# Where the first cross attention's vector work stands in order, and when the third expert weights are loaded

## The chip, the cores and the metric

The kernel runs on one core of one Trainium2 chip. The metric is device time in microseconds (us). An execution that is profiled also leaves a trace: for each engine, which instruction ran when. The engines are PE (TensorE, matrix products; PEld is its loading of weights), DVE (VectorE), ACT (ScalarE), POOL (GpSimd) and SP (SyncE, which here only issues DMAs). Each engine works through its own list of instructions, in an order that is fixed when the program is built.

## The reference: what is computed

Eight batches of 256 tokens with 256 features go through four blocks. Each block adds a gated cross attention to a context and then a gated feed-forward part:

```python
x = x + tanh(g_xattn[i]) * xattn_i(layernorm(x), ctx, ...)
x = x + tanh(g_ffn[i])   * ffn_i(layernorm(x), ...)
```

Block 0 has a cosine attention and a dense feed-forward part. Block 1 is the one that matters here: an attention of 16 heads with 16 features each, with the masked rows of the normalized input set to zero, and then a mixture of 8 experts. A router product gives 8 scores per token, the two greatest are kept, their exponentials are divided by their sum (the gates), and each kept expert computes `silu(x W1) * (x W2)`, 682 wide, times `W3`. Block 2 has an attention of 16 heads with 64 features and another mixture of 8 experts, with two shared experts beside it. Block 3 has two attentions.

## The kernel before

`x` stays on the chip, 16 tiles of 128 tokens (two tiles to a batch). The blocks follow one another.

**The attention of 16-wide heads** is `attention16` (L502), called for block 1 with `prologue` and `epilogue` from L813 and L837. It is a pipeline over 32 steps, four to a batch; a step does four heads. Step n, in the order of the code: `greatest` (L536) multiplies keys by queries (L525, tile `lg`) and has DVE take the greatest logit of each row, negated (L544, tile `nms`, two instructions); then the generators of the next batch's prologue and of the earlier batches' epilogues each advance by one `yield`; in every second step `shift` transposes the maxima (L556) and adds them to the queries (L558); `weights` multiplies again for a step three earlier (L525, tile `lb`) with the exponential on ACT (L570); and `values` multiplies by the values (L586) for a step four earlier. The logits, the second logits and the projections share three PSUM buffers (`psum2`, L49), so the second logits of a step wait until DVE has read the first ones.

The **prologue** of a batch has four parts: normalize x and transpose it (`ln_T`, L241: sums L207 and L208, variance L198, power -1/2 on POOL L200, row mask L219, apply L223, transposes L238 with ACT's copy L239); the queries (L675, DVE L822); the keys (ACT L828); the values (L685, ACT L689). The **epilogue** of a batch (from L837) begins four steps after the batch's last `greatest`: transposes (L606) and division by the row sums (`normalized`, L725 and L729), the residual (L841), the sums for the next norm (`norm_stats`); then `moe_token` (L735): the norm's apply and the store of the normalized tokens to DRAM by SP (L738), their transposes, the router product (L747, L751); then the two greatest scores (`top2_mask`, L755 to L770), and in a further step the gates (`l1_gates`, L778 to L787 and L801).

**Who sets the order.** The code's order is not the order of the lists. A planner in the tile framework simulates the program when it is built: on each engine it takes the earliest instruction of the code that is ready by its own estimate. An instruction that depends on little may so move ahead of others that stand before it in the code. The block `with behind(kind):` (L191) limits that: every instruction that the block issues on the engine of `latest[kind]` is put behind that instruction in the list. It adds no wait. `latest["maxima"]` is the last L544, `latest["norm"]` the last power on POOL. The second and the fourth attention use `behind` already, the first doesn't.

**The mixture of block 1** (L1069 to L1121). `places` (L858) makes from the mask, by a chain of small DVE instructions and three matrix products, the list of tokens for each of 39 slots of 128: first the place of each token, then one-hot rows (L925, four of them) whose products with PE (L930) give `token` (L935, L936), then the expert of each slot (L940 to L947). `l1_gates` for the last batch and `two_gates` (L959 to L973) make the two gates of each token. `routed` (L975) gathers the tokens of a slot with indirect DMAs from POOL (L982), transposes them (L992), multiplies by W1 and W2 (L1088), gates (ACT L1096, DVE L1098), transposes (L1009) and multiplies by W3 (L1106). W1 is loaded at the kernel's start (L109). W2 and W3 lie in a pool that is opened after the attention, so their DMAs on SP (L1071, L1074) wait until the attention's tiles are free. Block 2's mixture uses the same `places` and `two_gates`, with its shared experts' products beside them.

Of the kernel before, what the change touches and what calls it, by code (L numbers as in the profile page):

```python
# [8 lines left out]
F32 = mybir.dt.float32  # L9
# [26 lines left out]
def flamingo_kernel(ctx: ExitStack, tc: tile.TileContext, out: bass.AP, a: dict):  # L36
    nc = tc.nc

    const = ctx.enter_context(tc.tile_pool(name="const", bufs=1))
    w01_stack = ctx.enter_context(ExitStack())  # L40
    w01 = w01_stack.enter_context(tc.tile_pool(name="w01", bufs=1, side="right"))
    dram = ctx.enter_context(tc.tile_pool(name="dram", bufs=1, space=bass.MemoryType.DRAM))
# [79 lines left out]
    def gf(i):  # L122
        return gates[:, 4 + i : 5 + i]
# [37 lines left out]
        out=trip, in_=trip, compare_op=ALU.is_gt, fill=0.0, base=0,  # L161
        pattern=[[1, P]], channel_multiplier=-1,
    )
    count_i = const.tile([P, P], I32, name="count_i")
    nc.gpsimd.iota(count_i, pattern=[[1, P]], base=0, channel_multiplier=0)
    count = const.tile([P, P], F32, name="count")
    nc.vector.tensor_copy(count, count_i)
# [23 lines left out]
    def behind(kind):  # L191


        return tc.issue_after(latest[kind].ins)
# [16 lines left out]
    def norm_stats(b, name):  # L211
        mv = stats_of(x[:, 2 * b : 2 * b + 2, :], 2, name)
        return mv, rstd_of(mv, 2, name)
# [27 lines left out]
    def ln_T(b, name, rowmask=None):  # L241
        xn = layer_norm(b, name, rowmask)
        t = lnp.tile([P, 2, S], F32, tag="xnT", name=f"xnT_{name}")
        transposed(xn, t, name)
        return t
# [559 lines left out]
    with tc.tile_pool(name="l1x", bufs=2) as pl, tc.tile_pool(name="l1x1", bufs=1) as pl1:  # L805
        wq, wk, wv = l1x_w
        maskf = pl1.tile([P, NT], F32, name="maskf")
        nc.vector.tensor_copy(maskf, mask_u8)
        vas = spread_tiles(pl1, "l1")
        maxima = cleared_maxima(pl1, "l1")  # L810
        gcol = gx(1)

        def prologue(b):  # L813

            cx = ctx01[:, :, b * S : (b + 1) * S]
            xnT = ln_T(b, f"l1x{b}", rowmask=maskf[:, 2 * b : 2 * b + 2])
            qT = pl.tile([P, 4, S], F32, tag="qT", bufs=3, name=f"l1q{b}")
            kT = pl.tile([P, 4, S], F32, tag="kT", bufs=3, name=f"l1k{b}")
            yield
            for _, pp in project(wq, 2, lambda c: xnT[:, c, :], 2, f"l1pq{b}"):  # L820
                for u in range(2):
                    nc.vector.tensor_scalar(  # L822
                        of_half(qT, u), pp[:, 0:2, :], quarter[:, u : u + 1], None, ALU.mult
                    )
            yield
            for _, pp in project(wk, 2, lambda c: cx[:, c, :], 2, f"l1pk{b}"):
                for u in range(2):
                    nc.scalar.activation(  # L828
                        of_half(kT, u), pp[:, 0:2, :], AF.Identity,
                        bias=one_a[:, u : u + 1], scale=half[:, u : u + 1],  # L830
                    )
            yield
            va = vas[b % 3]
            values16(wv, lambda c, k: cx[:, c, k * P : (k + 1) * P], va, f"l1pv{b}")
            yield qT, kT, va

        def epilogue(b, av, st):  # L837
            att = pl.tile([P, 2, D], F32, tag="att", name=f"l1att{b}")
            normalized(av, 16, H, att, f"l1n{b}")
            xb = x[:, 2 * b : 2 * b + 2, :]  # L840
            nc.vector.scalar_tensor_tensor(xb, att, gcol, xb, ALU.mult, ALU.add)  # L841
            stats = norm_stats(b, f"l1f{b}")
            yield
            xT = lnp.tile([P, 2, S], F32, tag="xnT", name=f"xnT_l1f{b}")
            yield from moe_token(b, stats, l1xd, xT, l1_s, l1f_wg, "l1f")
            ts = slice(2 * b, 2 * b + 2)
            top2_mask(l1_s[:, ts, :], l1_mask[:, :, ts], f"l1g{b}", moe)
            if b + 1 < B:
                yield
                l1_gates(ts, f"l1g{b}")  # L850

        attention16("l1", pl, maxima, prologue, epilogue)

# [4 lines left out]
    def places(mask, name, pl1, kept):  # L858
# [63 lines left out]
        for k in range(4):  # L922
            ts = slice(k * NT // 2, (k + 1) * NT // 2)
            row = pl1.tile([P, NT // 2, P], BF16, tag=f"{name}row", name=f"{name}row{k}", bufs=2)
            nc.vector.tensor_tensor(  # L925
                row, count.unsqueeze(1).to_broadcast([P, NT // 2, P]),
                rc[:, 0, ts].unsqueeze(2).to_broadcast([P, NT // 2, P]), ALU.is_equal,
            )
            for t in range(k * NT // 2, (k + 1) * NT // 2):
                nc.tensor.matmul(  # L930
                    pi[:, : 2 * SP], row[:, t % (NT // 2), :], what[:, t].rearrange("p k s -> p (k s)"),
                    start=t == 0, stop=t == 2 * NT - 1,
                )
# [3 lines left out]

        at = pl1.tile([P, SP, E], F32, name=f"{name}at")
        edge = pl1.tile([P, E], F32, name=f"{name}edge")
        nc.vector.tensor_scalar_mul(edge, first[:, 0, :], 1.0 / P)  # L940
        nc.vector.tensor_tensor(
            at, edge.unsqueeze(1).to_broadcast([P, SP, E]),
            count[:, :SP].unsqueeze(2).to_broadcast([P, SP, E]), ALU.is_le,
        )
        expert_f = pl1.tile([P, SP], F32, name=f"{name}expert_f")
        nc.vector.tensor_reduce(expert_f, at, AX.X, ALU.add)
        nc.vector.tensor_scalar_add(expert, expert_f, -1.0)  # L947
        return slot, two

    def kept_tiles(pool, name):  # L950
# [115 lines left out]
    l1_kept = kept_tiles(const, "l1")  # L1066
    l1yd = dram.tile([SLOTS * P, D], F32, name="l1yd")
    l2x_pool, l2x_w = ExitStack(), {}
    with tc.tile_pool(name="l1w", bufs=1, side="right") as plw:  # L1069
        l1_w2 = plw.tile([P, E, 2, HID], F32, name="l1_w2")  # L1070
        nc.sync.dma_start(out=l1_w2, in_=a["l1f_w12"][:, :, :, HID:])  # L1071
        l1_w3 = plw.tile([P, E, NHC, D], F32, name="l1_w3")
        for e0 in range(0, E, 4):
            nc.sync.dma_start(out=l1_w3[:, e0 : e0 + 4], in_=a["l1f_w3"][:, e0 : e0 + 4])  # L1074
        l1_w12 = (l1_w1, l1_w2)
        token, expert, two_i, g2 = l1_kept
        with tc.tile_pool(name="l1p", bufs=1, side="right") as plp:
            slot, two = places(l1_mask, "l1g", plp, l1_kept[:3])
            l1_gates(slice(NT - 2, NT), "l1g_last")
            two_gates(l1_gate, slot, two, gf(1), g2, "l1g", plp)  # L1080
        with tc.tile_pool(name="l1f", bufs=2, side="right") as pl:
            def first_half(s, xT, e):
                ph = [psum2(f"l1ph{s}_{k}") for k in range(2)]
                for k in range(2):
                    for n in range(2):
                        o = n * HH
                        for c in range(2):
                            nc.tensor.matmul(  # L1088
                                ph[k][:, n, :HH], xT[:, c, :],
                                l1_w12[k][:, bass.ds(e, 1), c, o : o + HH].rearrange(  # L1090
                                    "p o n -> p (o n)"
                                ),
                                start=c == 0, stop=c == 1,
                            )
                sl = pl.tile([P, 2, HH], F32, tag="sl", name=f"l1sl{s}", bufs=1)
                nc.scalar.activation(sl, ph[0][:, :, :HH], AF.Silu)  # L1096
                h = pl.tile([P, HID], F32, tag="h", name=f"l1h{s}")
                nc.vector.tensor_tensor(  # L1098
                    h.rearrange("p (n h) -> p n h", n=2), sl, ph[1][:, :, :HH], ALU.mult
                )  # L1100
                return h

            def second_half(po, hT, e):
                for f in range(NHC):
                    n = min(P, HID - f * P)
                    nc.tensor.matmul(  # L1106
                        po, hT[:n, f, :],
                        l1_w3[:n, bass.ds(e, 1), f, :].rearrange("p o n -> p (o n)"),
                        start=f == 0, stop=f == NHC - 1,
                    )  # L1110

            def halfway():

                l1a_stack.close()
                pool = l2x_pool.enter_context(tc.tile_pool(name="l2x1", bufs=1))
                for n in ("l2x_wk", "l2x_wv", "l2x_wq", "l2x_wo"):
                    l2x_w[n] = load_w(n, pool)

            routed(
                l1xd, l1yd, token, expert, first_half, second_half, NHC, pl, "l1", halfway  # L1120
            )  # L1121


    l2w_stack = ctx.enter_context(ExitStack())
# [75 lines left out]
    with tc.tile_pool(name="l2r", bufs=1) as pl1, ExitStack() as l2s_stack:  # L1200
# [17 lines left out]
        pls = l2s_stack.enter_context(tc.tile_pool(name="l2s", bufs=2))  # L1218
        with tc.tile_pool(name="l2p", bufs=1) as plp:
            slot, two = places(mask2, "l2g", plp, l2_kept[:3])  # L1220
            nc.vector.tensor_tensor(gate2, gate2, mask2.rearrange("p e t -> p t e"), ALU.mult)
            two_gates(gate2, slot, two, gf(2), g2, "l2g", plp)


        l3x_w = [load_w(n, l3q) for n in ("l3x_wq", "l3x_wk", "l3x_wv", "l3x_wo")]
# [593 lines left out]
```

## Time and profile before

| what | us |
|---|---|
| median of 3 runs (lowest, highest) | 2085.5 (2084.23, 2093.49) |
| the profiled execution: time | 2085.53 |
| the profiled execution: span from first to last instruction | 2083.8 |
| PE busy (PEld) | 1897.0 (1249.8) |
| DVE, ACT, POOL busy | 1104.0, 682.9, 291.3 |
| mean granted TensorE clock | 0.955 |
| first maxima of the first attention | 216.93 |
| last residual of the first attention (L841), start | 439.83 |
| W2 asked for (L1071), W3 asked for (L1074) | 440.76, 443.78 |
| first gather issued, first slot's transposes on PE | 468.13, 474.75 |

The span and the granted clock come from the profile, the time from the run. The busy time of an engine doesn't say what bounds a stage; for that one looks at what ended the idle time before an instruction. In a line of the timeline the columns are: start, duration, engine, line of the kernel, operation, what it writes <- what it reads, shape, count; in brackets the idle time before it and whom it waited for. Neighbouring instructions of a kind are merged into one line.

### The profile page before, as it was taken

Reading aid. Unit: us, or ns where it says so; the run is one execution under the profiler, and the core shown is the slowest. Engines: PE = TensorE matmul, PEld = TensorE weight load, DVE = VectorE, ACT = ScalarE, POOL = GpSimd, SP = SyncE. Lnnn points to the kernel's source line nnn. Section 1 sums busy time; section 2 is a strip of 40 time slices with the busy share of each in tenths; the row PEclk is TensorE's granted clock in tenths of the full one; section 3 lists DMA queues with packets and bytes.
Section 4 is the critical chain, followed back from the end, with each engine's and each line's share of the span. In section 5 each row is a group of like instructions: output and inputs, shape, how many; then the busy total and the mean of one; then the engine's idle time right before and its main releaser. Section 6 shows DMA issues by size and latency. Waiting matters only on the chain. (4 is left out here: it accounts for less than half of the span.)

```text
span 2083.8 us, 31064 instructions
## 1 busy us (share of the span) xinstructions
PE 1897.0 (91%) x12226; PEld 1249.8 (60%) x12226; DVE 1104.0 (53%) x2193; ACT 682.9 (33%) x1467; POOL 291.3 (14%) x324
## 2 busy tenths in 40 slices
PE   6898988958999998999999999999878988899998
PEld 5565655635666665666666665566545554675665
DVE  4444656661111112566666774433378687647763
ACT  2221333422222221433343342012235454234443
POOL 2322000001111101211111102023221110610000
PEclk9999988978999999999999999999989899899999
DMA  9000000051111014000000003012322222000000
GB/s 261 1 1 0 1 11 11 11 216 57 33 31 34 29 26 182 26 16 16 16 16 15 13 3 129 11 59 87 88 87 81 87 72 82 1 1 6 11 11 16
DMA packets 44286, 96.67 MB, mean 46 GB/s; under 512 B 6992, under 2 KB 30256, under 8 KB 40816
## 3 DMA queue, kind: packets, MB, share of 16 engines
q1 hardware_dynamic: 34736, 75.25, 10.3%
q0 software_dynamic: 6816, 18.62, 3.3%
q8 instruction: 100, 1.64, 0.3%
q10 hardware_dynamic: 2592, 0.82, 0.3%
q14 instruction: 42, 0.34, 0.1%
HBM read 78.02 MB, written 16.65 MB: 45 GB/s over the span
## 5 line engine op out<-in xcount | busy, mean ns | idle before, releaser
L1088 PE MATMUL l1ph<-l_w,l1xT 128*128 x624 | 190.7, 458 | 0.0
L441 ACT ACTIVATE l2ex<-l2lg,l2nm 128x256 f32<-128x256 f32 x256 | 117.8, 472 | 204.8 <-DVE l2nm L437 201.2
L1088 PEld LDWEIGHTS l1ph<-l_w,l1xT 128*128 128x128 f32 x624 | 115.8, 190 | 66.5 <-issue 13.3
L1098 DVE TENSOR_TENSOR l1h<-l1sl,l1ph 128x682 f32<-128x682 f32 x39 | 33.8, 866 | 174.4 <-PE l1ph L1088 174.4
L1106 PE MATMUL l1po<-l_w,l1hT 128*128 x468 | 121.1, 388 | 0.0
L544 DVE TENSOR_REDUCE l1nms<-l1lg 128x4 f32<-128x1024 f32 x64 | 75.4, 1221 | 55.0 <-PE l1lg L525 55.0
L1477 DVE SCALAR_TENSOR_TENSOR l3ex<-l3ex,l3low 128x1024 f32<-128x1024 f32 x64 | 75.5, 1221 | 48.7 <-ACT l3ex L1471 41.2
L544 DVE TENSOR_REDUCE l3nms<-l4lg 128x4 f32<-128x1024 f32 x64 | 75.4, 1221 | 42.7 <-PE l4lg L525 42.6
L1106 PEld LDWEIGHTS l1po<-l_w,l1hT 128*128 128x128 f32 x468 | 79.7, 189 | 19.7 <-issue 13.3
L437 DVE TENSOR_REDUCE l2nm<-l2lg 128x4 f32<-128x1024 f32 x64 | 78.0, 1219 | 21.2 <-PE l2lg L431 20.6
L461 DVE COPY l2et<-l2tp 128x512 f32<-128x512 f32 x128 | 83.4, 681 | 2.6 <-PE l2tp L457 2.5
L570 ACT ACTIVATE l1ex<-l1lb 128x1024 f32<-128x1024 f32 x64 | 61.9, 1019 | 62.9 <-PE l1lb L525 62.2
L544 DVE TENSOR_REDUCE l3nms<-l3lg 128x4 f32<-128x1024 f32 x64 | 75.4, 1219 | 10.6 <-PE l3lg L525 10.4
L1096 ACT ACTIVATE l1sl<-l1ph 128x682 f32<-128x682 f32 x39 | 28.8, 739 | 153.9 <-PE l1ph L1088 153.9
L446 DVE TENSOR_TENSOR l2ex<-l2ex,l2z 128x1024 f32<-128x1024 f32 x64 | 78.1, 1221 | 1.5
L525 PE MATMUL l3lb<-l3q,l3k 32*128 32x256 f32 x512 | 62.0, 440 | 17.8 <-DVE l3nms L544 15.8
L431 PE MATMUL l2lg<-l2k,l2q 64*128 64x256 f32 x512 | 76.5, 402 | 0.4 <-ACT l2ex L441 0.4
L982 POOL DMA_INDIRECT l1xg<-l1xd,l1token x39 | 37.2, 954 | 281.6 <-PE l1xt L992 254.9
L570 ACT ACTIVATE l4ex<-l4lb 128x1024 f32<-128x1024 f32 x64 | 61.9, 1019 | 43.4 <-PE l4lb L525 43.0
L1471 ACT ACTIVATE l3ex<-l3lb 128x1024 f32<-128x1024 f32 x64 | 64.7, 1018 | 33.8 <-PE l3lb L525 33.8
L476 PE MATMUL l2av<-l2et,l2va 128*32 128x256 f32 x1024 | 74.4, 385 | 0.0
L457 PE MATMUL l2tp<-ident,l2ex 128*128 128x128 f32 x512 | 71.2, 279 | 3.4 <-DVE l2et L461 2.8
(740 smaller groups left out, 3796.6 us busy)
## 6 DMA issues: line engine op xcount, KB each, us to landing
l3low<-low_d SPq DMA_DIRECT2D x16, 1024.0 KB
l_w<-in_l1f_w SPq DMA_DIRECT2D x2, 5456.0 KB
l_w<-in_l1f_w SPq DMA_DIRECT2D x2, 3072.0 KB
l1yd<-l1y SPq DMA_DIRECT2D x39, 128.0 KB
l2yd<-l2y SPq DMA_DIRECT2D x39, 128.0 KB
l_w<-in_l2f_w SPq DMA_DIRECT2D x1, 4096.0 KB
x<-in_x SPq DMA_DIRECT2D x8, 256.0 KB
w_l0f_w<-in_l0f_w SPq DMA_DIRECT2D x2, 1024.0 KB
```

The lines of the kernel that those rows point to most:

```text
L431: nc.tensor.matmul(lg[:, j, i * S : (i + 1) * S], qT[r, p, i * P : (i + 1) * P], kT[r, p, :], start=True, stop=True,)
L437: latest["maxima"] = nc.vector.tensor_reduce(nm, lgv, AX.X, ALU.max, negate=True)
L441: nc.scalar.activation(ex[:, k, :], lgv[:, k, :], AF.Exp, bias=nm[:, k : k + 1], accum_out=z[:, k : k + 1],)
L446: nc.vector.tensor_tensor(ex, ex, z.unsqueeze(2).to_broadcast([P, 4, S]), ALU.mult)
L457: nc.tensor.transpose(tp[:, o : o + P], ex[:, 2 * j + i, k * P : (k + 1) * P], ident)
L461: nc.vector.tensor_copy(et, tp.rearrange("p (k n) -> p k n", k=2))
L476: nc.tensor.matmul(av[32 * j : 32 * j + 32, p % 4, :], va[:, k, 2 * p + j // 2, 32 * (j % 2) : 32 * (j % 2) + 32], pair[j // 2][:, k, :], ...
L544: latest["maxima"] = nc.vector.tensor_reduce(dst, lgv, AX.X, ALU.max, negate=True)
L570: nc.scalar.activation(exf, lbf, AF.Exp)
L1088: nc.tensor.matmul(ph[k][:, n, :HH], xT[:, c, :], l1_w12[k][:, bass.ds(e, 1), c, o : o + HH].rearrange("p o n -> p (o n)"), start=c == 0, ...
L1106: nc.tensor.matmul(po, hT[:n, f, :], l1_w3[:n, bass.ds(e, 1), f, :].rearrange("p o n -> p (o n)"), start=f == 0, stop=f == NHC - 1,)
L1477: nc.vector.scalar_tensor_tensor(exv, exv, 1.0, low.unsqueeze(1).to_broadcast([P, 2, 2 * S]), ALU.min, ALU.max)
```

## The change

In the first attention:

- from batch 1 on, all of `ln_T` in the prologue stands in `behind("maxima")`: sums, mask and apply come behind the maxima of the step in which the code issues them;
- the epilogue is cut into more steps. After the division it yields (but for the last batch); the residual and the sums come in the next step, behind its maxima; the apply of the norm and the token store in the step after; the transposes in the next; the router product in the next, with the mask behind that step's maxima; the gates in one more, behind theirs.

W3 has six chunks of 128 rows per expert. It was loaded in two transfers of four experts each after the attention. Now it is three tiles: chunks 0 and 1 in a pool on the right side of the memory that is opened at the kernel's start, loaded by a DMA in the prologue of batch 2; chunks 2 to 4 in a pool that is opened when the first context's pool is closed; and chunk 5 beside W2. `second_half` picks the tile by chunk.

In `places`, `latest["rows"]` is the last one-hot row, and the experts of the slots are computed behind it; so are, in both mixtures, the gates (`l1_gates` of the last batch and `two_gates` in block 1, the masking of the gates and `two_gates` in block 2). The integer tile for counting moves from the constants to a place that `top2_mask` uses later.

```diff
+    l1e = l1e_stack.enter_context(tc.tile_pool(name="l1e", bufs=1, side="right"))
+    l1_w3 = [l1e.tile([P, E, 2, D], F32, name="l1_w3a")]
...
-    count_i = const.tile([P, P], I32, name="count_i")
+    count_i = moe.tile([P, P], I32, tag="top_gt", name="count_i")
...
         def prologue(b):
+            if b == 2:
+                nc.sync.dma_start(out=l1_w3[0], in_=a["l1f_w3"][:, :, 0:2, :])
...
-            xnT = ln_T(b, f"l1x{b}", rowmask=maskf[:, 2 * b : 2 * b + 2])
+            with behind("maxima") if b else nullcontext():
+                xnT = ln_T(b, f"l1x{b}", rowmask=maskf[:, 2 * b : 2 * b + 2])
...
-            nc.vector.scalar_tensor_tensor(xb, att, gcol, xb, ALU.mult, ALU.add)
-            stats = norm_stats(b, f"l1f{b}")
+            if b + 1 < B:
+                yield
+            with behind("maxima"):
+                nc.vector.scalar_tensor_tensor(xb, att, gcol, xb, ALU.mult, ALU.add)
+                stats = norm_stats(b, f"l1f{b}")
             yield
             xT = lnp.tile([P, 2, S], F32, tag="xnT", name=f"xnT_l1f{b}")
-            yield from moe_token(b, stats, l1xd, xT, l1_s, l1f_wg, "l1f")
+            token = moe_token(b, stats, l1xd, xT, l1_s, l1f_wg, "l1f")
+            with behind("maxima"):
+                next(token)
+            yield
+            yield from token
             ts = slice(2 * b, 2 * b + 2)
-            top2_mask(l1_s[:, ts, :], l1_mask[:, :, ts], f"l1g{b}", moe)
+            with behind("maxima"):
+                top2_mask(l1_s[:, ts, :], l1_mask[:, :, ts], f"l1g{b}", moe)
             if b + 1 < B:
                 yield
-                l1_gates(ts, f"l1g{b}")
+                with behind("maxima"):
+                    l1_gates(ts, f"l1g{b}")
...
-            nc.vector.tensor_tensor(
+            latest["rows"] = nc.vector.tensor_tensor(
                 row, count.unsqueeze(1).to_broadcast([P, NT // 2, P]),
...
+        with behind("rows"):
+            nc.vector.tensor_scalar_mul(edge, first[:, 0, :], 1.0 / P)
...
-    with tc.tile_pool(name="l1w", bufs=1, side="right") as plw:
+    with (
+        tc.tile_pool(name="l1w3", bufs=1, side="right") as plw3,
+        tc.tile_pool(name="l1w", bufs=1, side="right") as plw,
+    ):
+        l1_w3.append(plw3.tile([P, E, 3, D], F32, name="l1_w3b"))
+        nc.sync.dma_start(out=l1_w3[1], in_=a["l1f_w3"][:, :, 2:5, :])
         l1_w2 = plw.tile([P, E, 2, HID], F32, name="l1_w2")
         nc.sync.dma_start(out=l1_w2, in_=a["l1f_w12"][:, :, :, HID:])
-        l1_w3 = plw.tile([P, E, NHC, D], F32, name="l1_w3")
-        for e0 in range(0, E, 4):
-            nc.sync.dma_start(out=l1_w3[:, e0 : e0 + 4], in_=a["l1f_w3"][:, e0 : e0 + 4])
+        l1_w3.append(plw.tile([P, E, 1, D], F32, name="l1_w3c"))
+        nc.sync.dma_start(out=l1_w3[2], in_=a["l1f_w3"][:, :, 5:6, :])
...
-            l1_gates(slice(NT - 2, NT), "l1g_last")
-            two_gates(l1_gate, slot, two, gf(1), g2, "l1g", plp)
+            with behind("rows"):
+                l1_gates(slice(NT - 2, NT), "l1g_last")
+                two_gates(l1_gate, slot, two, gf(1), g2, "l1g", plp)
...
             def second_half(po, hT, e):
                 for f in range(NHC):
+                    f0 = 0 if f < 2 else 2 if f < 5 else 5
+                    part = l1_w3[(0, 2, 5).index(f0)]
...
+    l1e_stack.close()
...
-            nc.vector.tensor_tensor(gate2, gate2, mask2.rearrange("p e t -> p t e"), ALU.mult)
-            two_gates(gate2, slot, two, gf(2), g2, "l2g", plp)
+            with behind("rows"):
+                nc.vector.tensor_tensor(gate2, gate2, mask2.rearrange("p e t -> p t e"), ALU.mult)
+                two_gates(gate2, slot, two, gf(2), g2, "l2g", plp)
```

## The prediction

> **What bounds the kernel now.** I read the busy shares first (PE 91%, DVE 53%, DMA far below), then PE's waits inside the first attention (205 to 441 us), then a table by stretches cut at the first step of each batch (start, length, PE, PEld, DVE, ACT, POOL busy, granted clock, DMA share, GB/s), then the timeline at one of the waits.
>
> ```profile
> PE l1lb L525 <- DVE l1nms L544: 17.6, 8, 3.3
> PE xt_l1x L238 <- DVE xn_l1x L223: 8.9, 2, 8.3
> ```
>
> ```profile
> 216.00:232.00 16.00, 14.63 (x127) 10.22 (x124) 11.89 (x13) 5.07 (x8) 0.00 (x0) 1.00 0.01 2
> 232.00:253.00 21.00, 21.00 (x232) 14.08 (x228) 12.03 (x12) 10.98 (x15) 0.00 (x0) 1.00 0.01 2
> 253.00:284.00 31.00, 27.28 (x252) 18.02 (x248) 19.52 (x44) 11.81 (x16) 1.39 (x2) 0.89 0.03 10
> 284.00:315.00 31.00, 27.62 (x256) 17.97 (x250) 19.51 (x44) 12.10 (x18) 1.39 (x2) 0.89 0.03 10
> ...
> 377.00:404.50 27.50, 25.95 (x250) 17.26 (x248) 17.88 (x37) 11.97 (x17) 0.69 (x1) 0.94 0.03 11
> 404.50:441.00 36.50, 29.37 (x350) 18.82 (x348) 25.16 (x65) 17.17 (x23) 1.39 (x2) 1.00 0.05 15
> 441.00:475.90 34.90, 8.57 (x54) 6.52 (x54) 18.91 (x59) 0.80 (x2) 5.04 (x6) 0.51 0.92 363
> ```
>
> ```profile
> 288.60 0.74 PEld L525 LDWEIGHTS l1lg<-l1k,l1q 32*128 32x128 f32 x16 [0.41 <-issue]
> ...
> 293.01 0.74 DVE L223 TENSOR_SCALAR xn_l1x<-x,mv_l1x,rp_l1x 128x256 f32<-128x256 f32 x2
> 293.66 2.35 DVE L544 TENSOR_REDUCE l1nms<-l1lg 128x4 f32<-128x1024 f32 x2
> ...
> 294.94 3.21 PE L525 MATMUL l1lb<-l1q,l1k 32*128 32x256 f32 x16 [3.26 <-DVE l1nms L544]
> ...
> 298.08 1.94 PE L586 MATMUL l1av<-l1ex,l1va 128*32 128x256 f32 x16
> ...
> 299.94 2.09 PE L525 MATMUL l1lg<-l1k,l1q 32*128 32x256 f32 x16
> ```
>
> A batch without an epilogue takes 21 us with PE full; one with an epilogue takes 31 us though its matmuls grew little. Once per batch a step's logits are finished at 289.7, but DVE first adds the residual, takes the sums of two batches and applies two norms, and comes to the maxima at 293.66. The logits' PSUM buffers are therefore not free, and PE stands for 3.26 us. Then it runs slow: 3.21, 1.94 and 2.09 us where the same groups took 1.39, 1.07 and 1.15 a step earlier, 1.82 + 0.87 + 0.94 = 3.6 us more, under a granted clock near half. Four such waits (264, 295, 326, 357 us) are 13.2 + 14.4 us; a smaller one at 385 is 1.5 + 2.0; one at 413 is 2.5 with no slowing. All that these waits can give is **33.6 us**.
>
> The second place is 441 to 476: PE nearly idle at clock 0.51, DVE building the token lists, the queues full of weights until 472. The first gather lands late.
>
> ```profile
> L982 POOL DMA_INDIRECT l1xg<-l1xd,l1token x39: 940/944/1295, 468.1 to 760.5; - x39
> ...
>   DMA l1xg<-l1xd,l1token: 8.1, 1
> ...
> DMA to landing us min/median/max: 2.7/2.8/6.5
> ```
>
> **Order of the maxima (the largest part).** The instructions are the same; what moves is DVE's order. Residual and sums go one step later and behind that step's maxima, the epilogue's norm a step after that, the router's mask and gates again later, and the next batch's norm behind the maxima of the step where its transposes are. Call the first step of a batch A and the others B, C, D.
>
> Step A. Maxima 2.36 us (284.13 to 286.49). Then the next batch's norm, now unable to run ahead: sums 0.75 + 0.30, variance 0.17, the power on POOL 0.70, mask 0.16, apply 0.74; the same chain without the mask ran from 429.45 to 432.24, so 3.0 with it. It ends at 289.5, or about 290.3 with some of normalize (0.35 + 0.74), shift (0.63) and mask work (about 1.7) between. PE meanwhile has the output transposes (to 285.9), the router product moved here (1.06), the shift's transposes (0.6), the weights' matmuls (1.39) and part of the values (1.07): to about 289. The norm's transposes, which sat ready at 284.39, become the point of a **new wait of about 1.3 us** (estimate, from these rows). Step A goes from 5.65 us (282.95 to 288.60) to 5.65 + 1.06 + 1.3 = 8.0.
>
> Steps B to D. DVE has maxima, q 1.40, residual 0.75, sums 1.2 and gates 1.0 in B: 6.8 us, less than a step and a half; C has 3.8, D 2.4. With no long wait they should run like the three steps from 235.41 to 251.88, 16.5 us, plus the epilogue's transposes 0.6 and 0.4 of leftover from B: 17.5. Now they take 25.3 (288.60 to 313.86). A batch: 8.0 + 17.5 = 25.5 instead of 30.9, **5.4 less**; four of these, 21.6. The batch at 377 goes from 27.5 to 25.5, 2.0. The wait at 413 goes, 2.5.
>
> What gets worse: batches 1 and 2 had their norms done early, in DVE's idle time. At 219.2 only an apply (0.73) lay between two maxima; now the whole chain does: +2.4. In the step at 231.25 PE has only 4.2 us of work and no epilogue: the chain ends at 234.4 + 3.0 = 237.4, so +3.1. Sum: -21.6 - 2.0 - 2.5 + 2.4 + 3.1 = -20.6.
>
> Clock after new waits: 3.1 us is like the rows that cost 3.6 more: +3.6. For the six waits near 1.3 us the rows disagree: 1.5 us at 385 was followed by 2.0 of slowing, 1.76 at 426.6 and 2.52 at 413 by none (clock 1.00 there). I take a third, 6 x 2.0 / 3 = 4.0, ends 0 and 12. **First attention: -20.6 + 3.6 + 4.0 = -13.0.**
>
> [...]
>
> **Third weights.** Chunks 0 and 1 (2,048 KB) are asked for at step 4, where the queues move 2 GB/s; chunks 2 to 4 (3,072 KB) when the first context's place is free; only w2 (5,456 KB) and the last chunk (1,024 KB) wait for the attention's end. At the 410 GB/s seen after 445, w2 and the last chunk take 16 us from 440.8, to about 457; with chunks 2 to 4 as late as that, 465. The gathers begin near 468. The first took 6.5 us to land against a median of 2.8: **-3.7**. Ends: 0 (if its length is a first gather's own) and -3.7. On SP the wait of w2 for the last residual (8.0 us behind L841) stays; the last token store is behind it as now. The second expert product is only at about 478, so w2 has cover; the first use of the third weights is at 494.
>
> **Gates behind the rows.** Twelve small instructions leave the chain from mask to rows. Where they filled DVE's gaps they were free (edge at 452.87 cost nothing); reading start to start, the chain loses 0.29 + 0.30 + 0.08 + 0.18 + 0.41 + 0.20 = **1.5 us**. They come back behind the last row, while PE multiplies the rows and the gathers fly (about 6 us); if two land ahead of the token copy it costs 0.4. In the third block the same 1.5 us lie on a chain for which PE waits at 1314.9 (1.29 us): -1.3; the later waits there are the rows' own. The shared experts' products behind them on DVE have 11.6 us of matmuls as cover.
>
> The counting tile's new place, the shift of pools by 16 KB and the split address of the third weights cost nothing that I see: the same number of matmuls, and the attention's zeroing already waits for the end of the layer before (203 us). If a pool now waits longer, it shows at 203 or 441. Between none and 3 us; I take none.
>
> **Sum.** The execution that was profiled took 2085.5 us (span 2083.8 and 1.7 around it), equal to the median of the runs. 2085.5 - 13.0 - 3.7 - 1.5 - 1.3 = 2066.0. I take **2066**.
>
> **Rivals.**
> Slower: the norm's transposes stand in PE's order ahead of the weights' matmuls. PE comes to them at 286.9, they are ready at 290: 3.1 us and 3.6 of slow clock in each of seven batches, 47, and 2.4 at the start, against 33.6 + 6.5 removed: +9.3, and with 1.2 more of delay to B's maxima **2096**. It decides where the wait passes some 3 us; for it, the four transposes came straight behind the logits at 284.39; against it, they were ready then, and now there is other work that is. 0.12.
>
> Given back: DVE's order in A and B leaves B's maxima late (A's work is 7.9 us for an 8.0 us step, nothing to spare), and the attention gains nothing. Only the 6.5 at the lists remain: **2079**. Also the answer if the new edges change little. 0.20.
>
> Everything: no new wait at all, 33.6 + 6.5 less: **2046**. 0.06.
>
> The forecast, 2055 to 2075, has 0.62. Faster by over 0.5% (below 2075, the least that a measurement of this kernel can tell from none) takes the forecast, "everything" and a little of "given back": 0.71. Slower by over 0.5%: 0.08, two thirds of the first rival. Within: 0.21. For 8 in 10 the range leaves out "everything" in part and the slower rival: 2050 to 2088.
>
> **What would show it.** Right: PE's wait for l1nms falls from 17.6 to under 5 us, a smaller wait for xn_l1x appears once per batch, stretches of 25 to 26 us, clock above 0.95 from 253 to 377; the first gather lands in about 3 us; the rows start 1.5 us earlier after the mask. Wrong: a wait of 3 us or more at xt_l1x each batch with clock 0.89, or maxima that still begin 3 us behind their logits, or w2 issued later than 1 us behind the last residual.

## The result, and the profile after

The changed kernel takes **2110.2 us** (median of 4 runs, 2106.8 to 2119.1) against 2085.7 (4 runs, 2084.2 to 2093.5): 1.014 times as long, 95% interval 1.0115 to 1.0165. The forecast was 2066, its range 2050 to 2088; the forecast was wrong in sign.

The profiled execution of the changed kernel is the longest of its four (2119.1, span 2117.2), 33.4 us of span above the one before. Read stage by stage, by the starts of the same instructions in both traces:

| stage | before | after | difference |
|---|---|---|---|
| start to first maxima (same order of instructions) | 216.9 | 220.5 | +3.5 |
| first maxima to last residual | 222.9 | 249.5 | **+26.6** |
| last residual to token list | 27.1 | 24.4 | -2.7 |
| token list to first gather's issue | 1.2 | 3.8 | +2.6 |
| issue to first slot's transposes | 6.6 | 3.2 | -3.4 |
| first to last slot's transposes | 320.9 | 328.8 | **+7.9** |
| the rest | 1288.1 | 1287.1 | -1.0 |

The first and the last row hold the same instructions in both kernels, but for the place of the gates and experts of block 2; over the 14 profiles of this study they range from 214.0 to 222.0 and from 1279.4 to 1290.3, so their differences say nothing about the change. Two stages carry the loss. For the attention, the waits of PE from 205 to 510 us, after (in us: sum, times, longest):

```profile
PE xt_l1x L241 <- DVE xn_l1x L226: 24.1, 9, 8.3
...
PE l1lb L528 <- DVE l1nms L547: 4.5, 11, 0.8
```

The big waits for the maxima are gone (17.6 before), and the new wait at the norm's transposes stands where the prediction put it; 8.3 of its 24.1 us are the attention's first batch, as before. But the waits are not where the time went. The stretch from first maxima to last residual, before and after (start:end, length, PE, PEld, DVE, ACT, POOL busy, granted clock, DMA share, GB/s):

```profile
216.93:439.83 222.90, 200.18 (x1928) 131.94 (x1928) 144.16 (x299) 92.82 (x122) 7.66 (x11) 0.93 0.03 9
```

```profile
220.46:469.98 249.52, 224.18 (x1928) 142.99 (x1924) 145.32 (x318) 92.98 (x122) 9.76 (x14) 0.87 0.06 21
```

PE is idle 22.7 us before and 25.3 after, nearly the same. The same 1928 matmuls take 24.0 us longer, under a lower clock. One batch of the timeline after shows how:

```profile
301.12 2.36 DVE L547 TENSOR_REDUCE l1nms<-l1lg 128x4 f32<-128x1024 f32 x2 [4.26 <-PE l1lg L528]
302.40 0.70 PE L528 MATMUL l1lb<-l1q,l1k 32*128 32x256 f32 x4 [0.29 <-DVE l1nms L547]
...
303.54 1.13 PE L528 MATMUL l1lb<-l1q,l1k 32*128 32x256 f32 x12 [0.43 <-DVE l1nms L547]
...
306.00 0.74 DVE L226 TENSOR_SCALAR xn_l1x<-x,mv_l1x,rp_l1x 128x256 f32<-128x256 f32 x2
...
306.47 0.87 PE L241 MATMUL xt_l1x<-ident,xn_l1x 128*128 128x128 f32 x4 [1.80 <-DVE xn_l1x L226]
...
307.18 1.56 PE L750 MATMUL l1fpg<-c_l1f_wg,xnT_l1f 128*128 128x8 f32 x8
...
312.01 1.94 PE L589 MATMUL l1av<-l1ex,l1va 128*32 128x256 f32 x16
...
313.87 2.08 PE L528 MATMUL l1lg<-l1k,l1q 32*128 32x256 f32 x12
```

DVE takes the maxima promptly at 301.12. PE waits 0.72 us in two parts for them, then 1.80 us for the norm, and from 307.35 its granted clock is 0.50: the router product takes 1.56 us (1.06 before), the values 1.94 (1.07). The clock's record in the trace has its switches on a fixed raster: in all 14 profiles of this study each switch lies a whole multiple of 3.413 us from the others, to 0.002 us (46 switches before, 54 after). Cut on that raster, the same batch reads (columns as above):

```profile
300.52:303.93 3.41, 2.69 (x32) 1.71 (x26) 2.81 (x4) 0.62 (x2) 0.00 (x0) 1.00 0.00 0
303.93:307.35 3.42, 1.61 (x19) 1.01 (x11) 2.29 (x10) 1.94 (x2) 0.70 (x1) 1.00 0.00 0
307.35:310.76 3.41, 3.41 (x14) 2.50 (x13) 0.96 (x4) 0.59 (x1) 0.00 (x0) 0.50 0.00 0
310.76:314.17 3.41, 3.41 (x23) 1.39 (x26) 1.35 (x4) 0.00 (x0) 0.00 (x0) 0.50 0.00 0
314.17:317.58 3.41, 3.41 (x16) 2.33 (x14) 2.40 (x4) 0.00 (x0) 0.00 (x0) 0.50 0.00 0
317.58:321.00 3.42, 3.42 (x39) 2.07 (x40) 2.95 (x9) 0.74 (x2) 0.00 (x0) 1.00 0.02 5
```

In the second stretch PE is busy 1.61 of 3.42 us, in pieces, and the clock is halved from its end for three stretches, 10.2 us. The 0.72 us at the second logits lie in the stretch before, which is busy 2.69 and is followed by a clock of 1.00; here the 1.80 us alone do it. After, all seven batches behind the first pay for such a stretch (busy shares 0.25 to 0.51), 6.8 to 13.7 us of half clock each, 64.9 us in all; before it was 30.7.

The slots are the other stage. The list after, and the first gather:

```profile
494.37 0.19 DVE L951 SCALAR_TENSOR_TENSOR l1token<-l1gpi,l1gpart 128x40 int32<-128x40 f32 x1
...
496.52 0.64 DVE L986 TENSOR_REDUCE l1g<-l1ghit 128x16 f32<-128x128 f32 x2
497.19 0.24 DVE L989 TENSOR_SCALAR l1g<-l1g,r_gates 128x32 f32<-128x32 f32 x1
498.14 1.30 POOL L998 DMA_INDIRECT l1xg<-l1xd,l1token  x1 [25.42 <-DVE l1g L989]
```

The gather has its tokens at 494.56 (494.37 + 0.19) and is issued at 498.14, behind the gates. The pool of the gathered rows is opened where the gates' work tiles were, so its first DMA has to wait for their last readers. And a slot in the middle, after:

```profile
606.45 0.38 PE L1008 MATMUL l1xt<-ident,l1xg 128*128 128x128 f32 x2
...
607.98 0.44 PE L1025 MATMUL l1ht<-ident,l1h 128*128 128x128 f32 x2 [0.27 <-DVE l1xT L1010]
...
615.39 0.38 PE L1008 MATMUL l1xt<-ident,l1xg 128*128 128x128 f32 x2
```

This slot lasts 8.94 us and PE idles 0.27 in it; others last 8.48. Of the slots in steady run 25 take 8.94 us after, 12 before. In each of these PE reads a slot's expert number into a register (an instruction of 0.30 us in the trace, not counted as busy); two slots of 8.48 us hold such a read too, 0.6 us earlier in the slot. Before, PE did 22 of these reads ahead of the first slot; after, 9 (count, then ns min/median/max, first and last start in us):

```profile
L995 PEldq TENSOR_LOAD <-l1expert x22: 295/299/495, 455.1 to 470.1; - x22
```

```profile
L1011 PEldq TENSOR_LOAD <-l1expert x9: 295/302/497, 494.7 to 500.4; - x9
```

### The profile page after: what moved, and what is told of

Read it like the earlier page. It is cut to its first block, busy times and chain, and to the rows that moved or that the text cites. A ratio compares the mean times of both kernels' runs of the same rounds, so it can differ in the third digit from the quotient of the medians.

```text
span 2117.2 us, 31075 instructions
## 1 busy us (share of the span) xinstructions
PE 1930.6 (91%) x12226; PEld 1266.1 (60%) x12226; DVE 1101.2 (52%) x2193; ACT 683.7 (32%) x1467; POOL 292.6 (14%) x324
## 3 DMA queue, kind: packets, MB, share of 16 engines
q1 hardware_dynamic: 37568, 75.25, 10.2%
## 5 line engine op out<-in xcount | busy, mean ns | idle before, releaser
L444 ACT ACTIVATE l2ex<-l2lg,l2nm 128x256 f32<-128x256 f32 x256 | 118.0, 473 | 204.9 <-DVE l2nm L440 201.4
L1497 ACT ACTIVATE l3ex<-l3lb 128x1024 f32<-128x1024 f32 x64 | 64.7, 1018 | 33.6 <-PE l3lb L528 33.6
L460 PEld LDWEIGHTS l2tp<-ident,l2ex 128*128 128x128 f32 x512 | 56.0, 141 | 29.8 <-issue 13.8
L1367 PE MATMUL l2ph<-l_w,l2xT 128*128 x156 | 73.3, 593 | 0.4 <-DVE l2xT L1010 0.4
```

The lines of the kernel that those rows point to most:

```text
L444: nc.scalar.activation(ex[:, k, :], lgv[:, k, :], AF.Exp, bias=nm[:, k : k + 1], accum_out=z[:, k : k + 1],)
L460: nc.tensor.transpose(tp[:, o : o + P], ex[:, 2 * j + i, k * P : (k + 1) * P], ident)
```

## The experiments

Each ratio is to the kernel before, run beside it on the same chip (its medians there 2080.3 to 2088.2). The columns for the first attention are from first maxima to last residual, in us.

| run | us | ratio (95%) | length | PE idle | PE busy | clock |
|---|---|---|---|---|---|---|
| before | 2085.7 | 1 | 222.9 | 22.7 | 200.2 | 0.93 |
| after | 2110.2 | 1.0140 (1.0115-1.0165) | 249.5 | 25.3 | 224.2 | 0.87 |
| e1 before, new attention | 2105.3 | 1.0111 (1.0056-1.0166) | 249.5 | 25.3 | 224.2 | 0.87 |
| e2 after, norm free | 2063.9 | 0.9918 (0.9889-0.9947) | 197.3 | 8.4 | 188.9 | 1.00 |
| e3 after, old epilogue | 2117.9 | 1.0165 (1.0122-1.0208) | 247.2 | 25.0 | 222.2 | 0.87 |
| e4 after, experts free | 2105.6 | 1.0109 (1.0065-1.0153) | 247.7 | 25.4 | 222.3 | 0.88 |
| e6 before, waits filled | 2075.2 | 0.9968 (0.9947-0.9989) | 216.9 | 15.4 | 201.4 | 0.97 |
| e7 norm and experts free | 2056.4 | 0.9885 (0.9843-0.9928) | 198.9 | 8.4 | 190.5 | 0.99 |
| e8 norm, experts, gates free | 2051.4 | 0.9847 (0.9816-0.9878) | 197.3 | 8.4 | 188.9 | 1.00 |
| e9 before, third weights | 2080.7 | 0.9995 (0.9972-1.0017) | 225.2 | 22.5 | 202.7 | 0.92 |
| e10 after, sums free | 2095.4 | 1.0064 (1.0034-1.0094) | 227.2 | 12.7 | 214.5 | 0.92 |
| e11 after, sums free, power behind | 2101.7 | 1.0091 (1.0067-1.0115) | 238.3 | 18.8 | 219.5 | 0.89 |
| e12 e10, router a step later | 2065.7 | 0.9895 (0.9831-0.9960) | 211.8 | 13.8 | 198.1 | 0.97 |
| e13 after, router a step later | 2095.8 | 1.0087 (1.0058-1.0117) | 236.1 | 26.0 | 210.1 | 0.90 |

### Which part of the attention's order (e1, e2, e3)

e1 is the kernel before with the two edits of the attention alone.

> The kernel before with only the first attention's new order: the prologue's norm behind the maxima and the cut epilogue. Loads, expert numbers and gates as before. Theory A (the new order costs the first attention 26.6 us between its first maxima and its last residual, 222.9 to 249.5 in the traces): the ratio to before is 1.010 to 1.015, 2107 to 2116 us. Rival B (the attention's loss is the lottery of the clock and the loss sits in the third weights and the gates): within 2080 to 2093.

Measured 1.0111, and the attention's length, idle and busy time are those of the changed kernel to 0.1 us. The loss of 26.6 is the order's; the load of 2 MB in the middle of the attention, which only the changed kernel has, doesn't show in it (249.5 us in both).

e2 takes one edge away:

```diff
-            with behind("maxima") if b else nullcontext():
-                xnT = ln_T(b, f"l1x{b}", rowmask=maskf[:, 2 * b : 2 * b + 2])
+            xnT = ln_T(b, f"l1x{b}", rowmask=maskf[:, 2 * b : 2 * b + 2])
```

> The changed kernel without one edge: the prologue's norm is free to run ahead again, the cut epilogue stays. Theory A1 (PE's wait at the norm's transposes, 24.1 us in 9, and the slow clock behind each, 5.4 us a batch, are the whole loss of the attention): no wait for xn_l1x beyond 1 us, stretches of a batch below 28 us, first attention under 225 us, ratio to before 0.985 to 1.003. Rival A2 (the cut of the epilogue costs, because values and shift come late): stretches stay above 31 us, ratio above 1.008.

Measured 0.9918: A1, with the attention far under its bound of 225. The stretch, and then the waits of PE from 205 to 510 us:

```profile
217.10:414.40 197.30, 188.93 (x1928) 125.57 (x1928) 137.19 (x297) 92.92 (x122) 7.65 (x11) 1.00 0.08 27
```

```profile
PE xt_l1x L241 <- DVE xn_l1x L226: 8.9, 2, 8.3
...
PE l1lb L528 <- DVE l1nms L547: 2.8, 6, 0.8
```

The clock is never halved from 213.5 to 414.9. The same 1928 matmuls take 188.9 us. A batch is 25.7 us. So beside the cut epilogue the edge on the norm costs 52 us of the attention (197.3 to 249.5), and the rest of the new order gains 25.6.

e3 has the norm's edge with the epilogue of before.

> The changed kernel with the epilogue of before; the prologue's norm stays behind the maxima. Theory A1 (the norm's edge is the loss): the wait for xn_l1x stays near 1.8 us or grows, since the residual and two sums are ahead of it again; first attention 245 to 260 us, ratio 1.010 to 1.025. Rival A2 (the epilogue's cut is the loss): first attention near 223, ratio near 1.00.

Measured 1.0165, length 247.2: A1 again. The cut of the epilogue brings nothing as long as the norm's edge is there. Beside the old epilogue the edge costs 24.3 us (222.9 to 247.2), not 52: the two edits don't add.

### The experts' place (e4)

```diff
-        with behind("rows"):
-            nc.vector.tensor_scalar_mul(edge, first[:, 0, :], 1.0 / P)
+        nc.vector.tensor_scalar_mul(edge, first[:, 0, :], 1.0 / P)
...
```

> The changed kernel with the experts of the slots free to be computed ahead of the rows, as before; the gates stay behind the rows. Theory C (PE reads the expert numbers into registers; before it does 22 of 35 ahead of time while the lists are built, after only 9, and a slot with its own read takes 8.94 us instead of 8.48): 13 x 0.46 = 6.0 us less than the changed kernel, about 2104 against 2110, and the slots of 8.94 fall from 26 to about 13. Rival D (the slower slots come from the third weights' three tiles): slots stay, 2108 to 2112.

The slots of 8.94 us fall from 25 to 10, those of 8.48 rise from 10 to 25, and the slot stage goes from 328.8 to 321.2 us, with the third weights in three tiles as they were: C, and D falls. 15 x 0.46 is 6.9 of the 7.6. In time it is 2105.6, where the list chain gave back 2.6 (24.4 to 27.0 from residual to token); its ratio's interval overlaps that of the changed kernel, so the gain is shown by the slots, not by the time.

### Filling the waits of the kernel before (e6)

```diff
+            junk = state.pop("junk", None)
+            if junk is not None:
+                for _ in range(20):
+                    nc.tensor.transpose(junk[:, :P], ident, ident)
             for u, lb in enumerate(four_rows(b, g, "lb", kT, qT)):
```

> The kernel before, with 20 useless 128x128 transposes (into a PSUM tile that nobody reads) put on PE just ahead of the second logits of the first step of batches 2 to 5, where PE stands 3.3 us for the maxima; they take about 2.7 us. The order of all other instructions is the same. Theory E (the slow clock follows from PE's own idle share in the 3.41 us stretch before, so idle time that is filled with useless work costs nothing more, and the slow matmuls behind it go): the wait falls to about 0.6 us, the second logits take 1.4 us instead of 3.2, a batch 27 us instead of 30.7, ratio to before 0.990 to 0.995. Rival F (the matmuls behind a wait are slow for another reason, such as their late operands): ratio 0.998 to 1.002.

Between the two: 0.9968. One batch of its timeline:

```profile
260.02 2.35 PE L569 MATMUL junk<-ident 128*128 128x128 f32 x20
262.30 1.15 PE L525 MATMUL l1lb<-l1q,l1k 32*128 32x256 f32 x16
...
268.90 0.70 PE L525 MATMUL l1lb<-l1q,l1k 32*128 32x256 f32 x4 [1.23 <-DVE l1nms L546]
270.03 1.13 PE L525 MATMUL l1lb<-l1q,l1k 32*128 32x256 f32 x12 [0.43 <-DVE l1nms L546]
271.09 1.72 PE L592 MATMUL l1av<-l1ex,l1va 128*32 128x256 f32 x16
```

E is right where the filler stands: no wait, and the second logits take 1.15 us instead of 3.2. Eighty useless transposes make the kernel faster. But then PE comes to the next step's second logits before DVE has their maxima, waits 1.66 us, and in two of four batches that halves the clock for one stretch of 3.41 us. A batch falls only from 30.9 to 28.2 to 29.8, and the attention by 6.0 us: half of the wait comes back in the next step, behind the same burst of work on DVE, which the 33.6 us that "these waits can give" had left out. The ratio lies between the two expectations.

### What each other part gives (e7, e8, e9)

e7 is e2 with the experts free as in e4; e8 in addition takes `behind("rows")` off the gates of block 1.

> The changed kernel with two edges taken away: the prologue's norm and the experts of the slots are free, as before. The sum of what each alone gave: the norm's edge about 46 us, the experts' 5 to 7: 2056 to 2060, ratio to before 0.986 to 0.991. If the two don't add (the expert numbers gain only because the clock of the list stage is slow), 2062 to 2066.

> As the last one, and the gates of the first mixture too stand where they did before, ahead of the rows. What the gates' place gives by the prediction: 1.5 us of the chain, so this is 1.5 slower than the last one. Theory G (the gathered rows land in the memory of the gates' work tiles, so behind the rows the gates hold the first gather, 2.4 to 2.9 us from the token list to its issue against 1.0): 1.5 to 2 us come back, so the two are within 1 us, and from the token list to the first gather it takes 1.0 us again.

e7 is 2056.4: they add in the traces, with an attention of 198.9 us and slots of 320.8; the interval of its ratio would also leave room for 2062 to 2066. In e8 the gather is issued 1.2 us behind the token list, in e7 2.6 (after: 3.8), and the list chain is as long in both (27.2 and 27.0): G, and the gates' place behind the rows gains nothing here. The two medians differ by 5.0 us, the traces from the last residual to the first gather's issue by 1.2; the intervals of the ratios overlap, so only the 1.2 is shown. **e8 beats both kernels**: 2051.4, ratio 0.9847 (0.9816 to 0.9878). It keeps the epilogue's cut, the third weights' loads and the gates of block 2.

e9 is the kernel before with the third weights alone.

> The kernel before with the third weights in three tiles and their early loads alone. The prediction's own term: the first gather lands in 2.8 to 3.3 us instead of 6.5, 3 to 4 us less, ratio 0.998 to 0.9985; slots of 8.48 and 8.94 us in the same number as before. Rival H (the split costs in the second product, or the early load of 2 MB collides with the attention): ratio 1.000 to 1.004.

From issue to the first slot's transposes 3.2 us instead of 6.6, slots as before (321.6 us, 12 of 8.94). The term is right in the trace; in time 0.9995 (0.9972 to 1.0017) can't tell 3.4 us from none. The attention, whose order is that of before, is 2.3 us longer here: the stretches at 409 and 423 us, busy 0.51 and 0.49, were followed by half clock, and their like before, at 411 and 425, busy 0.53 and 0.50, were not. Where the raster falls is luck of this size.

### What halves the clock (e10 to e13)

e10 leaves sums, variance and power free and holds mask and apply only; e11 holds the power too:

```diff
+            stats = norm_stats(b, f"l1x{b}")
             with behind("maxima") if b else nullcontext():
-                xnT = ln_T(b, f"l1x{b}", rowmask=maskf[:, 2 * b : 2 * b + 2])
+                xn = norm_apply(b, stats, f"l1x{b}", maskf[:, 2 * b : 2 * b + 2])
...
```

> The changed kernel, with the sums, the variance and the power of the prologue's norm free to run ahead; only mask and apply stay behind the maxima. Theory J (PE waits because the whole chain of 3.0 us comes behind the maxima, while PE has only 1.2 us of work left when they end; mask and apply are 0.9): no wait for xn_l1x beyond 0.2 us from batch 3 on, batches of 25.7 us as with the edge taken away, 2060 to 2068, ratio 0.990 to 0.994. Rival K (an edge on the norm as such costs, or the free sums hold up maxima as they did before): batches of 28 us or more, 2075 and above, ratio above 0.997.

> As the last one, but only the sums are free: the variance, the power on POOL, mask and apply stay behind the maxima, a chain of 1.9 us. Theory J: PE's wait for xn_l1x is 0.5 to 0.8 us a batch instead of 1.8. Whether the clock pays: with the 0.7 us at the second logits PE is idle 1.3 us of a 3.41 us stretch, busy 0.62, where stretches so far went either way; without slow stretches a batch is 26.3 to 26.8 us and the time 2066 to 2074, with one in each batch 29 to 30 and 2088 to 2096. Rival K as above: 2075 and above with the waits elsewhere than at xn_l1x.

My theory J had e10 right in the waits and wrong in the time: no wait for xn_l1x from batch 3 on, PE idle only 12.7 us in the whole attention. Its batches are 24.9 and 25.2 us as long as no epilogue's router product stands in the step, then three times 30.8, and the ratio is 1.0064. K has the time, but the waits elsewhere that it asks for are not there: 4.5 us at the second logits, as after. In e11 the waits are those that J gave (8.4 us in 7); its batches are 26.5 and 26.1, and then 31.9 to 33.1, longer than either branch of the expectation. On the raster e10 shows why:

```profile
318.06:321.48 3.42, 2.99 (x21) 2.12 (x22) 2.65 (x8) 0.59 (x1) 0.00 (x0) 1.00 0.00 0
321.48:324.89 3.41, 3.41 (x16) 1.67 (x20) 2.21 (x8) 0.15 (x1) 0.00 (x0) 0.50 0.00 0
324.89:328.30 3.41, 3.41 (x32) 1.61 (x24) 0.06 (x1) 1.78 (x2) 0.00 (x0) 0.50 0.00 0
```

The clock is halved after a stretch in which PE is busy 2.99 of 3.42 us. The same stretch for the router product alone (PE, PEld, DVE busy):

```profile
318.06:321.48 3.42, 0.96 (x8) 0.97 (x8) 0.04 (x1) 1.00 0.00 0
```

0.96 us of it are eight matmuls that move 8 columns each. The new theory M, an assumption so far: what counts is the work in the stretch, and these products add little to it, busy as they are. e12 moves them by one step and nothing else on PE in batches 3 to 7:

```diff
             yield
+            next(token)
+            yield
+            if b + 1 < B:
+                yield
             yield from token
```

> The kernel of the run with the sums free, with the epilogue's router product one step later (one more yield): on PE nothing else changes its place in batches 3 to 7 but these four or so 8-column products, which leave the step of the norm's transposes. That run has no wait above 0.5 us, and yet PE's clock is halved for 6.8 us in each batch, after a stretch of 3.41 us that is busy 0.87, of which 0.28 are these narrow products (0.59 without them), and its batch is 30.8 us. Theory M (the clock goes by how much work the array gets in fixed stretches of 3.41 us; narrow products count next to nothing, short waits add up): without the products the stretch has 0.6 plus 0.28 of full matmuls, the clock stays, a batch is 25.7 us, 2066 to 2074, ratio 0.991 to 0.997. Rival N (the short waits at the second logits alone, 0.72 us, or the order of transposes and second logits, make the clock fall): a batch stays near 30.8, 2090 to 2100.

```profile
338.48:341.90 3.42, 2.70 (x24) 1.47 (x18) 2.97 (x6) 0.46 (x1) 0.00 (x0) 1.00 0.00 0
341.90:345.31 3.41, 3.41 (x40) 2.14 (x42) 1.63 (x4) 1.94 (x3) 0.00 (x0) 1.00 0.00 0
```

2.70 us busy, less than in e10, without narrow products: the clock stays at 1.00. PE is idle more than in e10 (13.8 against 12.7), its matmuls take 16.4 us less, a batch is 26.4 us, the ratio 0.9895 (0.9831 to 0.9960). A lucky place on the raster doesn't explain it: 26.4 us is no multiple of 3.413, so each batch falls elsewhere, and the least busy stretches, 0.79 to 0.89, were all spared. N falls. The medians are 30 us apart (2095.4 and 2065.7); the traces show 15.4 of this in the attention (227.2 to 211.8). Another 9.5 lie in the rest behind the slots, where the code is the same and other profiles differ as much; what makes them is open.

e13 makes the same move in the changed kernel.

> The changed kernel itself, with the router product one step later as in the last run, and nothing else. Theory M for the change as it was made: there PE is idle 2.5 us of the stretch (0.72 at the second logits, 1.80 for xn_l1x), so without the narrow products the stretch is still only 0.3 to 0.5 busy and the clock still falls in each batch; a batch goes from 33.2 to 31 to 33, ratio 1.007 to 1.013, 2098 to 2110. Rival P (in the changed kernel too the narrow products are what pulls the clock down, and the wait would pass unpunished): a batch of 28 us or less, 2085 and below, ratio under 1.001.

1.0087, batches of 29 to 30: P falls, and M has the ratio, though not the batch of 31 to 33. The clock is still halved in every batch: the stretches ahead of it are busy 0.35 to 0.56 without any narrow product, so the waits are enough alone. The half clock falls from 64.9 to 47.8 us and a batch by about 3 us; the narrow products, all that was moved, no longer stand in the slow stretch.

## Why the prediction was wrong, step by step

- **What the waits cost now (33.6 us): right in place, incomplete.** The waits for the maxima went as said. e6 shows that DVE's burst stands close behind; spreading DVE's work, which the epilogue's cut does in e2, makes the attention 25.6 us shorter.
- **Step A, the chain of 3.0 us and a wait of 1.3: the chain right, PE's cover not.** The chain lets PE go on 3.0 us behind the maxima. The sum had the router product, the shift's transposes, the second logits and part of the values ahead of the norm's transposes; in the trace only the second logits are, with 1.2 us left when the maxima end, and the wait is 1.80 in the five later batches. That it is not longer still is luck: the 0.8 us by which the sum lets other work delay the chain did not come. A further 0.72 at the second logits was not in the sum; PE no longer has transposes to do there.
- **Steps B to D and a batch of 25.5: near the order without the norm's edge, partly by luck.** e2 and e8 have 25.7, but without the wait of 1.3 us that the 25.5 include.
- **Start of the attention (+2.4, +3.1): right in kind.** The waits there are 3.73 and 2.50 us, and each goes with a clock of 0.50, for 6.8 and 10.2 us.
- **The clock after new waits (+3.6 and "a third, 6 x 2.0 / 3 = 4.0, ends 0 and 12"): this step failed.** With 16.4 us of slowing gone, the sum had matmuls 8.8 us shorter than before; they are 24.0 us longer. That is 32.8 of the 39.6 us between the forecast for the attention (-13.0) and the result (+26.6); the other 6.8 are the rest, 4.2 us less by the sum and 2.6 us more of PE's idle time in the trace. I priced each wait as an event of its own, by rows that disagreed (385 against 413 and 426), and took a share of them. The raster tells more than the length of a wait: the 2.52 us at 413 fell into two stretches, busy 0.73 and 0.53, and the wait at 385 left its stretch of 3.413 us busy 0.56. Yet it doesn't settle these rows: 0.56 was followed by half clock, 0.53 and, for the wait at 426, 0.50 were not. All three lie in the range that goes either way. In the new order the 1.80 us fall into one stretch in each of the five later batches, in some with a part of the 0.72, and leave it busy 0.34 to 0.49; in the 14 profiles every stretch as idle as that was followed by half clock.
- **Third weights (-3.7): right,** -3.4 after and -3.4 alone in e9.
- **Gates behind the rows (-1.5 in block 1): wrong by what was not seen.** The list chain did get 2.7 shorter, nearly all by the experts' move (e7 keeps the gates behind and has 27.0). Its price was not in the sum: 13 register reads of PE moved into the slots, 13 x 0.46 = 6.0 of the 7.9 us there, and the gather held by the gates' memory, 2.6. The prediction named what hides the gates (the flying gathers) and not what the gathers themselves wait for. In block 2 PE's waits for the token list went from 4.7 to 2.6 us in the traces, and a new one of 0.9 for the experts came in: 1.2 less, against the 1.3 given.
- **The slower rival** (2096, 0.12) had the right place, PE standing at the norm's transposes in every batch with slow clock behind, and the right sign. Its order was not quite that: the second logits stand ahead of the transposes. It asked for a wait of 3.1 us, and 1.8 was enough. The rival "everything" comes to 2045.4 by its own terms, not 2046.

How idle the stretch was ahead of a half clock differs widely: after the change PE is idle 1.8 of 3.413 us in the stretch shown, in e10 only 0.43, and the granted clock is 0.50 behind both.

What stays open: the exact measure. For every stretch at full clock from 213 to 440 us in the 14 profiles I took PE's busy share. All 43 under 0.495 were followed by half clock. From 0.495 to 0.69 it was 28 of 35. Those spared hold values, projections or transposes beside the logits, but so do some that were not; what sets them apart is not shown. Above, only the four of e10 were, of 681; some forty stretches that are full but hold 0.24 to 0.31 of narrow products were spared. In these runs half clock followed idle time and, in the four of e10, thin matmuls with less idle time; how much each weighs is not settled.

## What to carry to other kernels

Cut the timeline of PE on the raster of its clock (3.413 us in these traces) before pricing a wait: a wait, or a short wait with thin matmuls, that emptied one stretch cost more here in slow matmuls behind it than it lasted (1.80 us of wait and 10.2 us of half clock in the batch shown; 0.43 us idle and 6.8 us of half clock in e10). An order that keeps a ready transpose in front of a wait as cover was worth keeping here: put behind an edge only what holds up the chain (here the epilogue, 25.6 us less in e2), not what the cover needs (here the norm, 52 us more beside the cut epilogue). When a value moves later, look for its scalar readers and for whose memory it keeps: here the register reads (13 x 0.46 = 6.0 us) and the pool that opens in the same place (2.6 us) cost more than the chain gained (2.7 us).

## What the runs showed of the hardware that was not expected

- PE's granted clock switched only on a raster of 3.413 us in these 14 profiles, and stayed at half for one to four stretches (3.4 to 13.7 us) in this attention.
- It was halved after stretches that were 0.85 to 0.87 busy, when 0.27 to 0.28 of them were 8-column products (e10, four of four); and eighty useless transposes (9.4 us) shortened a kernel, by 0.3% (0.1 to 0.5).
- A register read by PE in the loop of the slots cost 0.46 us (8.94 against 8.48) in 25 of the 27 slots in steady run that hold one, though the read itself lasts 0.30.
